# One copy of the 7x7 filter band from HBM per channel group instead of two, and the second half of the partitions filled by VectorE

## The chip, the cores and the metric

The kernel runs on one NeuronCore of one Trainium2 chip. The metric is device time in microseconds of the whole program, from its first to its last instruction. Three runs of the kernel before took 5907.85, 5908.91 and 5926.22 us; the median is 5908.91 us. The profiled execution, from which all lines below come, spans 5915.1 us at a mean granted TensorE clock of 0.979 of full speed.

## The reference

Two convolution blocks in float32 on x of shape 8 x 96 x 96 x 192 (batch, height, width, channels), each with a group norm in front and a residual around it. The change touches the depthwise 7x7 convolution of the second block only.

```
# layer 0
x = x + _L0_conv_ref(_gn(x), ...)   # 192->384 projection, 3x3 depthwise, 4 scans, layer norm, 384->192
# layer 1
x = x + _L1_conv_ref(_gn(x), ...)

def _L1_conv_ref(x, dw_kernel, dw_bias, ...):
    y = conv(x, dw_kernel, SAME, feature_group_count=192) + dw_bias   # 7x7, one filter per channel
    y = (y - mean(y)) * rsqrt(var(y) + 1e-6) * ln_gamma + ln_beta     # over channels
    y = gelu(y @ w0 + b0) @ w1 + b1
    return y * gamma
def _gn(v):   # 32 groups of 6 channels, mean and variance over height, width, group
```

## The kernel before

The program runs as five stages, each with pools of its own, which hand their results on through HBM: A (group norm and projection), B (3x3 convolution and scans), C (layer norm, output projection, residual, statistics of the second group norm), D (the 7x7 convolution), E (layer norm, two-layer perceptron, residual). Only stage D is changed. It lasts from about 2938 us, where its first loads are issued, to about 3459 us, where stage E reads its result.

Stage D computes the convolution as matmuls against a banded matrix. A row of the image tensor X1_d in HBM is a pair of image row and width phase (width modulo PH = 3). A window of HB = 21 image rows times 3 phases gives KB = 63 partitions to contract over. Six such windows (NB) overlap so that each yields 15 image rows, 45 partitions of output. They sit in two halves of the 128 partitions: windows with g = 0 in partitions 0 to 63, those with g = 1 in 64 to 127, three of each (NT). The filter of each channel is laid out beforehand, in HBM tensor Z2_d, as a band of 64 rows and ZW = 208 columns; three 64-column slices of it (d = 0, 1, 2) are the stationary matrices. **The same band serves both halves[...], so the band has to lie in both halves.**

The 192 channels are 32 groups m of HC = 6 channels. `load_d(m)` issues the loads of one group: six DMAs of 384 KB for `xin` (line 753), of which the three with g = 0 go to SyncE's queue and those with g = 1 to GpSimd's, and two DMAs of 312 KB for `band` (line 758), one on each queue, which read the same bytes of Z2_d. `scale_d(m)` applies the second group norm to `xin` in place with eight VectorE instructions (line 1015). `conv_d` takes a pair of groups, m = 2i and 2i + 1 (k = 0 and 1 in the code), and runs channel by channel: 36 matmuls (3 windows t, 3 slices d, 2 groups k, 2 halves g), each of which the profile records as two, and then four ScalarE instructions that move the sums from PSUM to `yo` with the bias added (line 1041). `store_d` writes a finished pair to Y_d (line 1067): the half of group k = 0 by SyncE's queue, that of k = 1 by GpSimd's.

The order is written by hand (`tc.manual_schedule()`). For pair i it is: stores of pair i - 1 for k = 0; loads of groups 2i + 3 and 2i + 4; stores of pair i - 1 for k = 1; scaling of groups 2i + 2 and 2i + 3; the matmuls of pair i. There are five buffers each for `xin` and `band` (ND = 5), so group 2i + 3 takes the buffers of group 2i - 2 and can be read only when pair i - 1 is computed. There are two buffers `yo`, so the sums of pair i can be moved only when the stores of pair i - 2 have landed. Group 0 is read while stage C still ends, groups 1 and 2 at the start of stage D.

Of the kernel before, what the change touches and what calls it, by code (L numbers as in the profile page):

```python
# [84 lines left out]
def conv_blocks_kernel(  # L85
# [31 lines left out]
    nc = tc.nc  # L117
# [26 lines left out]
    HC = GS  # L144
# [19 lines left out]
    Z2_d = dram.tile([64, D, ZW], F32, name="Z2_d")  # L164
# [58 lines left out]
    with ExitStack() as ph:  # L223
# [247 lines left out]
        with tc.manual_schedule():  # L471
# [13 lines left out]
            for b in range(B):  # L485
                more = b + 1 < B
                for t in range(n_t):
# [28 lines left out]
                    k, j = divmod(t, NJ)  # L516
# [27 lines left out]
    with ExitStack() as ph:  # L544
# [13 lines left out]
        def load_b(k):  # L558
            c = slice(k * CC, (k + 1) * CC)
            band = bp_.tile([128, CC, 3, RB], F32, tag="band", name=f"band0_{k}")  # L560
            pin = bp_.tile([128, CC, GB, NJ, S], F32, tag="pin", name=f"pin_{k}")
            for g in range(NG):
                p = g * 64
                nc.sync.dma_start(
                    band[p : p + RB + 4].rearrange("p c t o -> p (c t o)"),
                    ZB_d[:, c].rearrange("r c t o -> r (c t o)"),
                )
                for lo, hi in ((0, RB), (RB, RB + 1), (RB + 1, RB + 2)):
                    nc.sync.dma_start(
                        pin[p + lo : p + hi].rearrange("p c b j h -> p c (b j h)"),  # L570
                        P_d[g, c, lo:hi].rearrange("c r b j h -> r c (b j h)"),
                    )
            return band, pin
# [71 lines left out]
        with tc.manual_schedule():  # L645
            loads = [load_b(k) for k in range(3)]
# [8 lines left out]
            for n in range(NI * (n_k + 1)):  # L655
                k, i = divmod(n, NI)
                z = None
                if k < n_k:
                    if i == 0:
                        band, pin = loads.pop(0)  # L660
# [79 lines left out]
    def load_d(m):  # L740
        c = m * HC
        row = D * WV * B
        pool = d_pools[m % ND > 0]
        xin = pool.tile([128, NT, BP, HC, 2 * WV], F32, tag="xin", name="xin")

        for t in range(NT):
            for g, eng in enumerate((nc.sync, nc.gpsimd)):
                src = bass.AP(
                    tensor=X1_d.tensor,
                    offset=X1_d.offset + (2 * t + g) * HG * PH * row + c * WV * B,  # L750
                    ap=[[row, 64], [1, HC * WV * B]],
                )
                eng.dma_start(
                    xin[g * 64 : (g + 1) * 64, t].rearrange("q a c n -> q (a c n)"), src
                )
        band = pool.tile([128, HC, ZW], F32, tag="band", name="band1")
        for g, eng in enumerate((nc.sync, nc.gpsimd)):
            eng.dma_start(
                band[g * 64 : (g + 1) * 64].rearrange("q c l -> q (c l)"),
                Z2_d[:, c : c + HC].rearrange("r c l -> r (c l)"),  # L760
            )
        return band, xin

    s1 = s1_pool.enter_context(tc.tile_pool(name="s1", bufs=1)).tile(
# [2 lines left out]
    with ExitStack() as ph:  # L767
# [179 lines left out]
        with tc.manual_schedule():  # L947
            load_weights()
            for u in range(n_u + 1):
# [22 lines left out]
                if held is not None:  # L972
                    k, t = divmod(u - 1, n_c)
# [8 lines left out]

            stores.pop(0)()
            first_d = load_d(0)
            for store in stores:
                store()
# [10 lines left out]
    with ExitStack() as ph:  # L997
        cp = ph.enter_context(tc.tile_pool(name="d_const", bufs=1))
        d_pools[1] = ph.enter_context(tc.tile_pool(name="d_in", bufs=ND - 1))
        op = ph.enter_context(tc.tile_pool(name="d_out", bufs=2))  # L1000
        ps_y = ph.enter_context(tc.tile_pool(name="d_ps", bufs=4, space=PSUM))

        dwb = cp.tile([128, D // CD, HC], F32, name="dwb")
        for k in range(2):
            nc.scalar.dma_start(
                dwb[k * 64 : (k + 1) * 64],
                dw_bias.rearrange("(i k c) -> k i c", k=2, c=HC)[k].partition_broadcast(64),
            )

        def scale_d(m, xin):  # L1010
            xv = xin.rearrange("q t a c (v b) -> q t a c v b", b=2)
            for b in range(B):
                sc, sh = (s1[:, a, b % 2, b // 2, m : m + 1] for a in range(2))
                xw = xv[:, :, b // 2, :, :, b % 2]
                nc.vector.tensor_scalar(xw, xw, sc, sh, ALU.mult, ALU.add)  # L1015

        def conv_d(pair, c, yo, i):

            pys = [
                [ps_y.tile([128, 2, BP, 2 * WV], F32, tag=f"py{a}", name=f"py{a}")  # L1020
                 for _ in range(2)]
                for a in range(2)
            ]
            for t in range(NT):
                for n, d in enumerate((1, 0, 2)):
                    lo, hi = 2 * max(0, 1 - d), 2 * (WV - max(0, d - 1))
                    for k in range(2):
                        for g in range(2):
                            rows = slice(g * 64, g * 64 + KB)
                            nc.tensor.matmul(  # L1030
                                pys[t // 2][g][k * 64 : (k + 1) * 64, t % 2, :, lo:hi],
                                pair[k][0][rows, c, d * ZS : d * ZS + 64],
                                pair[k][1][rows, t, :, c, lo + 2 * (d - 1) : hi + 2 * (d - 1)],
                                start=(n == 0),
                                stop=(n == 2),
                            )
                if t == 0:
                    continue
                for g in range(2):
                    bl = slice(g, 4 + g, 2) if t == 1 else slice(4 + g, 5 + g)  # L1040
                    nc.scalar.activation(
                        yo[:, bl, :, c],
                        pys[t // 2][g][:, : 2 - t // 2].rearrange("q t b (a v) -> q t (b a) v", a=NV),
                        AF.Identity,
                        bias=dwb[:, i, c : c + 1],
                        scale=1.0,
                    )

        def store_d(yo, i, k):

            eng = (nc.sync, nc.gpsimd)[k]

            w = BP * NV * HC * 2 * WQ
            n = NV * HC * 2 * WQ if i == D // CD - 1 else w
            for at in range(0, w, n):
                for bl in range(NB):

                    pieces = [(3, HB - 3)]
                    if bl == 0:
                        pieces.append((HB - 3, HB))  # L1060
                    if bl == NB - 1:
                        pieces.append((0, 3))
                    for lo, hi in pieces:
                        r = (S - HB - bl * HG) * PH
                        src = yo[k * 64 + lo * PH : k * 64 + hi * PH, bl]
                        dst = Y_d[r + lo * PH : r + hi * PH, 2 * i + k]
                        eng.dma_start(  # L1067
                            dst.rearrange("r b a c n -> r (b a c n)")[:, at : at + n],
                            src.rearrange("r a c n -> r (a c n)")[:, at : at + n],
                        )  # L1070

        n_i = D // CD
        with tc.manual_schedule():
            loads = [first_d] + [load_d(m) for m in range(1, 3)]
            make_weights(ps_y.tile([128, 512], F32, tag="py1", name="ps_b0"))
            for m in range(2):
                scale_d(m, loads[m][1])
            done = None
            for i in range(n_i):
                pair, loads = loads[:2], loads[2:]  # L1080

                if done is not None:
                    store_d(done, i - 1, 0)
                for m in (2 * i + 3, 2 * i + 4):
                    if m < 2 * n_i:
                        loads.append(load_d(m))
                if done is not None:
                    store_d(done, i - 1, 1)
                if i + 1 < n_i:
                    for k in range(2):  # L1090
                        scale_d(2 * i + 2 + k, loads[k][1])
                done = op.tile([128, NB, BP * NV, HC, 2 * WQ], F32, tag="yo", name=f"yo_{i}")
                for c in range(HC):
                    conv_d(pair, c, done, i)
            for k in range(2):
                store_d(done, n_i - 1, k)
# [246 lines left out]
```

## Time and profile before

| Stage | us | PE busy | VectorE busy | GpSimd busy | mean DMA share | GB/s |
|---|---|---|---|---|---|---|
| A, 0 to 780 | 780 | 712.77 | 412.96 | 111.33 | 0.85 | 245 |
| B, 780 to 1835 | 1055 | 1027.33 | 988.04 | 826.14 | 0.91 | 237 |
| C, 1835 to 2938 | 1103 | 1075.60 | 762.03 | 723.69 | 0.87 | 256 |
| D, 2938 to 3459 | 521 | 417.81 | 166.28 | 149.23 | 0.95 | 303 |
| E, 3459 to 5915 | 2456 | 2417.89 | 1125.46 | 751.17 | 0.27 | 70 |

The numbers are the busy time of each engine in a stretch of the span, in us. The DMA share is the mean busy share of the core's 16 DMA engines and the last column what they moved. In four of the five stages TensorE is busy for more than nine tenths of the time. In stage D it is busy for 418 of 521 us, and the DMA engines are the busiest resource. Stage D is 8.8% of the span, and a hundredth of the whole time is 59 us, so what can be won or lost there is small against the whole.

### The profile page before, as it was taken

What the parts mean: (1) busy time and instruction counts of PE and PEld (TensorE: products, weight loads), DVE (VectorE), ACT (ScalarE), POOL (GpSimd) and SP (SyncE); (2) the same over time, 40 slices, a digit from 0 to 9 for tenths busy, and PEclk for the clock granted to TensorE, in tenths of its full rate; (3) what the DMA queues carried; (4) which work ended last, traced back from release to release, by engine and by line L of the source; (5) the groups of instructions that cost most, each with busy time, mean ns of one, the idle gap of its engine ahead of it and who ended that gap; (6) DMA issues with size and microseconds to landing.
All of it is one profiled execution on the core that took longest, in us unless ns stands there. A gap on an engine that the chain in (4) does not pass through costs nothing.

```text
span 5915.1 us, 122868 instructions
## 1 busy us (share of the span) xinstructions
PE 5651.4 (96%) x48550; PEld 3971.6 (67%) x48550; DVE 3454.8 (58%) x8023; ACT 2429.1 (41%) x6146; POOL 2561.6 (43%) x2731
## 2 busy tenths in 40 slices
PE   6999989999998999999878869999999999999999
PEld 3655533333335989898767757777777777777777
DVE  5555459999996667777733334444444444444443
ACT  2444447777775555555434322222222222222221
POOL 1111138888886666666522223323333333333332
PEclk9999989999999999999989989999999999999999
DMA  7999779999997889888899952232323232323221
GB/s 205 279 284 262 217 211 244 244 245 244 243 243 201 256 262 267 262 266 262 240 317 332 316 130 74 63 77 64 80 65 81 64 80 65 80 60 81 63 65 39
DMA packets 634283, 1054.49 MB, mean 178 GB/s; under 512 B 108683, under 2 KB 509284, under 8 KB 633708
## 3 DMA queue, kind: packets, MB, share of 16 engines
q1 hardware_dynamic: 516924, 620.81, 40.3%
q0 software_dynamic: 110656, 423.20, 22.0%
q8 instruction: 384, 6.29, 0.5%
q10 hardware_dynamic: 6128, 2.61, 0.2%
q14 instruction: 191, 1.56, 0.1%
HBM read 585.19 MB, written 476.72 MB: 180 GB/s over the span
## 4 chain that ended last, share of the span: by engine, by line
PE 78%; DMA 5%; issue 1%; DVE 1%; POOL 1%; SPq 0%; ACT 0%; ACTq 0%; POOLq 0%; DVEq 0%
PE po L1232 19%; PE po L835 14%; PE hp L1202 12%; PE pl L582 10%; PE hp L1212 7%; PE pa L603 5%; PE pt L833 4%; PE py L1030 3%; DMA xin<-X_d 3%; PE pa L606 2%; PE pt L1185 2%; DMA Y_d<-yo 2%; DMA X_d<-x1c 0%; DMA P_d<-po 0%; SPq L1067 0%
## 5 line engine op out<-in xcount | busy, mean ns | idle before, releaser
L1221 ACT ACTIVATE g<-hp,b0g 128x384 f32<-128x384 f32 x1152 | 564.4, 589 | 1830.5 <-PE hp L1212 1830.5
L1232 PE MATMUL po<-w1g,g 128*128 128x192 f32 x6912 | 1160.0, 327 | 0.0
L1232 PEld LDWEIGHTS po<-w1g,g 128*128 128x128 f32 x6912 | 1118.8, 190 | 1.1 <-issue 1.1
L835 PE MATMUL po<-wc,mt 128*96 128x193 f32 x4608 | 912.8, 333 | 0.0
L1189 DVE COPY yT<-pt 128x384 f32<-128x384 f32 x288 | 251.0, 871 | 1043.3 <-PE pt L1185 1043.1
L1202 PE MATMUL hp<-yT,w0w 128*128 128x384 f32 x2304 | 781.4, 489 | 0.4 <-DVE yT L1189 0.4
L835 PEld LDWEIGHTS po<-wc,mt 128*96 128x96 f32 x4608 | 701.8, 163 | 68.2 <-ACT mean L839 64.8
L1250 POOL DMA_DIRECT2D out_dram<-xo x576 | 342.9, 597 | 875.4 <-DVE xo L1239 860.6
L582 PE MATMUL pl<-pin,band 34*32 34x380 f32 (+1 forms) x13824 | 629.7, 489 | 18.5 <-DMA pin<-P_d 18.5
L1202 PEld LDWEIGHTS hp<-yT,w0w 128*128 128x128 f32 x2304 | 429.5, 191 | 257.2 <-issue 3.2
L612 DVE TENSOR_TENSOR_SCAN z<-decay,loc 128x768 f32<-128x768 f32 x288 | 505.9, 1757 | 60.1 <-ACT loc L591 30.7
L652 POOL TENSOR_TENSOR mo<-mo,z 128x768 f32<-128x768 f32 x288 | 530.1, 1841 | 3.4 <-ACT mo L607 0.4
L29 POOL TENSOR_TENSOR rs<-rs_ve,neg_half 96x8 f32<-96x8 f32 x96 | 159.2, 1659 | 824.1 <-DVE rs_ve L28 804.0
L582 PEld LDWEIGHTS pl<-pin,band 34*32 34x32 f32 x13824 | 232.7, 107 | 397.5 <-issue 396.2
L621 DVE TENSOR_TENSOR_SCAN z<-decay,z 128x768 f32<-128x768 f32 x288 | 498.3, 1730 | 0.0
L1030 PE MATMUL py<-xin,band 63*64 63x248 f32 (+1 forms) x6912 | 409.5, 392 | 74.7 <-DVE xin L1015 46.3
L842 ACT ACTIVATE sq<-pt,mean 96x384 f32<-96x384 f32 x768 | 443.5, 578 | 25.7 <-ACT mean L839 0.8
L1030 PEld LDWEIGHTS py<-xin,band 63*64 63x64 f32 x6912 | 354.4, 141 | 129.5 <-DVE xin L1015 36.5
L603 PE MATMUL pa<-loc,mix 128*32 128x384 f32 x3456 | 431.9, 493 | 0.0
L606 PE MATMUL pa<-last,down 96*32 96x384 f32 x1152 | 426.8, 493 | 1.0 <-ACT mo L607 1.0
L1212 PE MATMUL hp<-yT,w0w 64*128 64x384 f32 x2304 | 423.5, 500 | 0.0
L365 PE MATMUL pm<-xT,win 128*128 128x384 f32 x1152 | 395.8, 494 | 5.2 <-DVE po L389 5.2
(116 smaller groups left out, 7621.5 us busy)
## 6 DMA issues: line engine op xcount, KB each, us to landing
P_d<-po POOLq DMA_DIRECT2D x96, 1152.0 KB, 9.6
pin<-P_d SPq DMA_DIRECT2D x192, 576.0 KB
mt<-M_d SPq DMA_DIRECT2D x576, 192.0 KB
xq<-in_x_dram SPq DMA_DIRECT2D x96, 576.0 KB
xr<-in_x_dram SPq DMA_DIRECT2D x384, 144.0 KB
X_d<-x1u POOLq DMA_DIRECT2D x192, 288.0 KB, 4.2
X_d<-x1c SPq DMA_DIRECT2D x192, 288.0 KB
y<-Y_d SPq DMA_DIRECT2D x24, 2304.0 KB
```

The lines of the kernel that those rows point to most:

```text
L582: nc.tensor.matmul(pls[g][at * RB : (at + 1) * RB, :, lo:hi], band[rows, c, kh, :], pin[rows, c, :, NJ - 1 - j, lo + kh - 1 : hi + kh - 1] ...
L603: nc.tensor.matmul(pa[at], mix[:, i, at], loc[:, q], start=True, stop=True)
L606: nc.tensor.matmul(pa[at], down[:, to], last[:, q], start=True, stop=True)
L612: nc.vector.tensor_tensor_scan(zf, decay_f, loc.rearrange("p q n -> p (q n)"), 0.0, ALU.mult, ALU.add)
L621: nc.vector.tensor_tensor_scan(zr, decay_f, zr, 0.0, ALU.mult, ALU.add)
L652: nc.gpsimd.tensor_tensor(m, m, z, ALU.add)
L835: nc.tensor.matmul(po[:S, b], lhs[m], wc[:, m], start=(m == 0), stop=(m == NC - 1))
L1030: nc.tensor.matmul(pys[t // 2][g][k * 64 : (k + 1) * 64, t % 2, :, lo:hi], pair[k][0][rows, c, d * ZS : d * ZS + 64], pair[k][1][rows, t, ...
L1202: nc.tensor.matmul(hps[m, q], w0w[:, 2 * q, m * 128 : (m + 1) * 128], yT[:, 2 * q], start=True, stop=False,)
L1212: nc.tensor.matmul(hps[m, q], w0w[p, 1, m * 128 : (m + 1) * 128], yT[p, 1], start=False, stop=True,)
L1221: nc.scalar.activation(g[:, m, q], hps[m, q], AF.Gelu, bias=b0g[:, m : m + 1], scale=1.0)
L1232: nc.tensor.matmul(po[:, q], g[:, m, q, k * 128 : (k + 1) * 128], w1g[:, m], start=(m == 0), stop=(m == NE - 1),)
```

## The change

Of the two DMAs for a group's band, one is left: group m reads it into the half g = m % 2, on that half's queue, so that even groups use SyncE's queue and odd groups GpSimd's and each queue carries one band per pair. The other half is filled by one VectorE copy of 64 partitions by 1248 elements, ahead of the scaling of that group. The purpose is to read each band from HBM once and to load both queues alike.

```diff
         band = pool.tile([128, HC, ZW], F32, tag="band", name="band1")
-        for g, eng in enumerate((nc.sync, nc.gpsimd)):
-            eng.dma_start(
-                band[g * 64 : (g + 1) * 64].rearrange("q c l -> q (c l)"),
-                Z2_d[:, c : c + HC].rearrange("r c l -> r (c l)"),
-            )
+
+        g = m % 2
+        (nc.sync, nc.gpsimd)[g].dma_start(
+            band[g * 64 : (g + 1) * 64].rearrange("q c l -> q (c l)"),
+            Z2_d[:, c : c + HC].rearrange("r c l -> r (c l)"),
+        )
         return band, xin
...
-        def scale_d(m, xin):
+        def scale_d(m, band, xin):
+            g = m % 2
+            nc.vector.tensor_copy(
+                band[(1 - g) * 64 : (2 - g) * 64], band[g * 64 : (g + 1) * 64]
+            )
             xv = xin.rearrange("q t a c (v b) -> q t a c v b", b=2)
...
-                scale_d(m, loads[m][1])
+                scale_d(m, *loads[m])
...
-                        scale_d(2 * i + 2 + k, loads[k][1])
+                        scale_d(2 * i + 2 + k, *loads[k])
```

## The prediction

> **What bounds the kernel now.** I first split the span into stretches, to find what limits the 7x7 stage, which alone is changed. The columns are length, busy time of each engine (with instruction counts), granted clock, DMA share, GB/s.
>
> ```profile
> 3050.00:3100.00 50.00, 44.22 (x761) 40.22 (x757) 18.41 (x31) 21.47 (x42) 14.39 (x28) 0.93 1.00 339
> 3100.00:3150.00 50.00, 45.67 (x800) 38.39 (x796) 15.21 (x26) 23.82 (x47) 14.61 (x27) 0.93 1.00 336
> 3300.00:3350.00 50.00, 42.91 (x694) 35.27 (x690) 13.22 (x23) 20.62 (x41) 14.06 (x26) 0.90 1.01 312
> 3400.00:3450.00 50.00, 41.41 (x714) 39.67 (x706) 4.74 (x8) 22.53 (x44) 12.47 (x25) 0.91 0.56 165
> ```
>
> The DMA engines are busy without a break (share 1.00) until the loads run out near 3400; PE, at 43 to 46 of 50 us, is next. VectorE has over 30 us free in each 50. So bytes set the pace, and PE is close behind. The second view is TensorE in order of time: start, length, records, and in brackets the idle time before.
>
> ```profile
> 2965.72 1.19 PE L1030 MATMUL py<-xin,band 63*64 63x256 f32 x4 [6.49 <-DVE xin L1015]
> 2981.80 49.24 PE L1030 MATMUL py<-xin,band 63*64 63x256 f32 x864 [14.89 <-DVE xin L1015]
> 3036.36 25.63 PE L1030 MATMUL py<-xin,band 63*64 63x256 f32 x432 [5.33 <-DVE xin L1015]
> 3064.12 25.44 PE L1030 MATMUL py<-xin,band 63*64 63x256 f32 x432 [2.13 <-DVE xin L1015]
> 3093.21 24.52 PE L1030 MATMUL py<-xin,band 63*64 63x256 f32 x432 [3.65 <-DVE xin L1015]
> ...
> 3368.38 25.41 PE L1030 MATMUL py<-xin,band 63*64 63x256 f32 x432 [5.54 <-ACT yo L1041]
> 3398.36 32.96 PE L1030 MATMUL py<-xin,band 63*64 63x256 f32 x567 [4.57 <-ACT yo L1041]
> ```
>
> One pair of groups is 6912/16 = 432 records. Pairs 0 and 1 run as one block (49.24 us, 24.6 each), since their data is there. From pair 2 on PE stops in every pair, first for scaled inputs, from pair 9 on mostly for ScalarE. The idle times of this view from 2981.8 on add up to 53.4 us: all that a faster supply could win. The period of a pair is that from pair 2 at 3036.36 to pair 15 at about 3415.6 (3398.36 plus the 292 records left of pair 14 at some 59 ns): 379.2/13 = 29.17 us. Third, who waits for whom (total us, times, longest):
>
> ```profile
> DVE xin L1015 <- DMA Y_d<-yo: 174.8, 11, 19.6
> DVE xin L1015 <- DMA xin<-X_d: 89.2, 16, 16.6
> ACT yo L1041 <- DMA xin<-X_d: 78.1, 8, 11.9
> PE py L1030 <- DVE xin L1015: 46.3, 13, 14.9
> PE py L1030 <- ACT yo L1041: 23.7, 6, 5.5
> ```
>
> PE waits for VectorE, VectorE for DMAs. ScalarE neither reads xin nor writes it; I read its wait for a DMA as one for the store of pair i - 2 out of its buffer yo, put down to whatever landed last. Both are waits for one DMA pool.
>
> **What the Trainium skill says.** "VectorE: DVE Perf Modes", section "The perf-mode tier table": an fp32 copy from SBUF to SBUF runs at two elements a cycle, 1227 ns for 2048. That is 1067 ns of streaming and 160 fixed. The trace of before has no contiguous copy of this kind; the nearest, the weight scaling of 128x768, three of which take 1.67 us or 557 ns from start to start, agrees (768/1.92 + 160 = 560 ns). "SBUF — State Buffer", section "Who interferes with whom": such a copy shuts GpSimd out of a shared port, also while it writes DMA descriptors. No line of before shows it; a GpSimd DMA issue takes about 510 ns here. "DMA: Bandwidth & Descriptors", section "Rules for kernel authors": transfers to two halves of the partitions share the same 16 DMA engines. The trace agrees: two queues are open and the share stands at 1.00. So dropping one half's band saves its bytes in full, on whichever queue it was.
>
> **The change part by part.** *Removed:* 32 of these 64 DMAs.
>
> ```profile
> xin<-X_d POOLq DMA_DIRECT2D x94, 384.0 KB, 14.0
> Y_d<-yo POOLq DMA_DIRECT2D x90, 270.0 KB, 13.6
> band<-Z_d SPq DMA_DIRECT2D x32, 312.0 KB
> band<-Z_d POOLq DMA_DIRECT2D x32, 312.0 KB, 16.9
> ```
>
> A group reads 6 x 384 + 2 x 312 = 2928 KB and writes 6 x 270 + 2 x 54 = 1728 KB (the 54 KB pieces are the image's edge rows), so a pair moves 9312 KB. At 29.17 us that is 327 GB/s, within the 312 to 339 of the stretches. Now it moves 8688 KB, 0.933 of it. If the DMA engines stay the limit at the same rate, the period becomes 27.22 us, still above PE's 24.6 to 25.6; the saving is 1.95 us in each of 13 periods, **25.4 us**. After pair 15 nothing is read, so the tail only moves earlier. The 32 issues (about 0.5 us each) go too, beside a full DMA queue: nothing.
>
> *Added:* 32 copies of 64x1248. By the page 1248/1.92 + 160 = 810 ns; at one element a cycle (the scaling here, 576 strided elements in 666 ns) it would be about 1360 ns. I take 0.81: 26 us in all, 43 at the other end, in a stage where VectorE is idle for some 350 us. On its own path it is one link: loads land, copy, scaling (4.75 us for eight), PE. While DMA is the limit a link of 0.8 us costs nothing, because the queued stores and loads of another group keep the DMA engines busy meanwhile.
>
> *The new wait:* the copy stands ahead of the scaling and waits for the band, which is issued after its group's xin. Behind it on VectorE queue the eight scalings, and for those PE. For odd groups in the steady state the band is on GpSimd's queue, whose loads come before its stores, while half of xin on SyncE's queue comes after 1728 KB of stores, so xin is last: nothing. For even groups the band closes SyncE's loads, some 2 us later than xin; they are scaled a whole pair ahead (3039.39 for pair 3, which starts at 3064.12): nothing. Only the start has no slack. Group 1's xin had landed at 2976.8 and scaling began at 2976.95. Its band, 312 KB on one queue at half of some 320 GB/s, comes about 2.0 us later; with the copy, PE starts pair 0 some **2.8 us later**. Against that, groups 1 to 5, which pair 2 waits for, bring 5 x 312 KB less, 4.9 us at 327 GB/s; but pair 0's end, which lets group 5 be read, comes later by the 2.8, and the DMA engines run dry in between. For pair 2 I count a net loss of 1.4 us, the middle between nothing and the 2.8.
>
> *GpSimd locked out:* at most 0.8 us per copy for an issue that has a full queue behind it: nothing.
>
> **Sum:** -25.4 + 1.4 = -24.0; 5908.9 - 24.0 = **5885 us**.
>
> **The rivals.** (1) *Supply still limits, but less well overlapped.* When PE and DMA are nearly level, a wait for a buffer idles both: PE must finish a pair before the next loads start, and yo is freed only by stores queued behind loads. For it: from pair 9 on PE waits for ScalarE at rates of 312 to 318 GB/s, so order already costs something. If PE keeps about 2.6 us of idle time per pair on 25.5, the period is 28.1 us and the gain 13 x 1.07 - 1.4 = 12.5: **5896 us**. Against it: the share of 1.00, a full queue, even then. (2) *The late waits vanish.* With fewer bytes before them the stores land in time and the later pairs run at the 336 GB/s of the stretches around 3100: 8688 KB in 26.5 us, a gain of 13 x 2.67 = 34.7, less 1.4: **5876 us**. For it: pairs 2 to 8 did so. Against it: nothing shows what set off the change at pair 9. (3) *The copy takes the place of the read.* If the pace is set by the chain of load, copy, scaling and PE, and fewer bytes bring no group earlier, then one copy per pair (0.81 to 1.36) lies on it: 15 x 1.1 + 2.8 = 19 us more, **5928 us**. For it: PE's commonest wait is for the scaling. Against it: that scaling itself waits 12 to 20 us for DMAs.
>
> **How the numbers follow.** Forecast 0.57, rival 1 0.20, rival 2 0.17, rival 3 0.06. The bound of 0.3% is 17.7 us. Faster: nearly all of the forecast (0.53), rival 2 (0.17) and a little of rival 1 (0.03), 0.73. Within: most of rival 1 and the rest, 0.22. Slower: 0.05. The range, 5870 to 5900, takes in the forecast, rival 2 and the better half of rival 1, and the two ends of the copy's price (at 1.36 us only the start moves, by 0.5 us); it leaves out rival 3 and the far ends of 1 and 2.
>
> **What would show it.** Right: stage D shorter by some 24 us and no other stage changed; DMA share near 1.00 to the end of the loads; a period near 27.2 us; PE's idle time down to some 30 us; the copy near 0.8 us; first long block of PE at about 2984.6. Rival 1 shows in a DMA share below 0.97 in mid-stage, rival 2 in the loss of waits for ScalarE, rival 3 in VectorE waiting for band rather than xin. I am wrong if the rate in GB/s falls with the bytes: then requests, not bytes, were the limit.

## The result and the profile after

The changed kernel takes 5881.5 us (median of 4 runs, 5878.4 to 5886.1) against 5912.6 us before (4 runs, 5907.9 to 5926.2) in the same comparison. The ratio is 0.9944, with a 95% interval of 0.9925 to 0.9963: some 31 us less. The profiled execution spans 5881.8 us, 33.3 us less than the one of before. All but about 1 us of that lies in the 7x7 stage: stages A, B and C together end 1.3 us earlier, and stage E takes as long as before.

The same four stretches as in the prediction, in the columns length, busy times, granted clock, DMA share, GB/s:

```profile
3050.00:3100.00 50.00, 45.28 (x796) 41.12 (x792) 21.56 (x35) 23.13 (x44) 15.77 (x28) 0.93 0.98 336
3100.00:3150.00 50.00, 45.00 (x824) 38.36 (x820) 22.19 (x36) 23.01 (x44) 16.15 (x28) 0.97 0.98 332
...
3300.00:3350.00 50.00, 46.54 (x812) 38.02 (x812) 20.10 (x33) 22.80 (x44) 15.21 (x28) 0.97 0.99 326
...
3400.00:3450.00 50.00, 11.12 (x205) 7.66 (x197) 5.62 (x20) 6.52 (x13) 17.84 (x33) 0.65 0.75 174
```

In the first three stretches the DMA engines are still busy nearly all the time, at 326 to 336 GB/s, where before the rate fell to 312 late in the stage. The last stretch is already past the end of the convolution. TensorE in order of time, with the idle time before each block in brackets:

```profile
2981.96 43.71 PE L1035 MATMUL py<-xin,band 63*64 63x256 f32 x789 [15.47 <-issue]
3026.27 4.45 PE L1035 MATMUL py<-xin,band 63*64 63x256 f32 x75 [0.60 <-issue]
3035.14 25.23 PE L1035 MATMUL py<-xin,band 63*64 63x256 f32 x432 [4.42 <-DVE xin L1020]
...
3248.99 48.69 PE L1035 MATMUL py<-xin,band 63*64 63x256 f32 x864 [3.95 <-DVE xin L1020]
...
3356.83 24.81 PE L1035 MATMUL py<-xin,band 63*64 63x256 f32 x432 [3.64 <-DVE xin L1020]
3383.08 8.33 PE L1035 MATMUL py<-xin,band 63*64 63x256 f32 x148 [1.44 <-DVE xin L1020]
3394.02 16.70 PE L1035 MATMUL py<-xin,band 63*64 63x248 f32 x280 [2.61 <-issue]
```

Pair 2 starts at 3035.14 and pair 15 at 3383.08, so the period is 347.94/13 = 26.76 us, 2.41 us less than the 29.17 of before; 13 of them are 31.3 us. The block of 864 records shows two pairs that ran on without a stop. The idle times from the first block on add up to 38.7 us, against 53.4. Who waits for whom:

```profile
DVE band L1013 <- DMA band<-Z_d: 127.5, 29, 11.8
DVE xin L1020 <- DMA Y_d<-yo: 106.9, 13, 10.2
...
PE py L1035 <- DVE xin L1020: 32.8, 11, 7.5
...
PE py L1035 <- ACT yo L1046: 0.2, 1, 0.2
```

VectorE's long wait is now split: first for the band, then, once it has copied, for the rest of xin (the line names a store, but what the scaling needs is xin). TensorE's wait for ScalarE, 23.7 us before, is gone. The copy itself, with the shortest, median and longest duration in ns:

```profile
L1013 DVE COPY band<-band x32: 802/805/879, 2959.7 to 3371.8; 64x1248 f32<-64x1248 f32 x32
```

### The profile page after: what moved, and what is told of

It reads as the page before. It is cut to its first block, busy times and chain, and to the rows that moved or that the text cites. A ratio compares the mean times of both kernels' runs of the same rounds, so it can differ in the third digit from the quotient of the medians.

```text
span 5881.8 us, 122840 instructions
## 1 busy us (share of the span) xinstructions
PE 5632.6 (96%) x48550; PEld 3954.1 (67%) x48550; DVE 3480.6 (59%) x8055; ACT 2431.2 (41%) x6146; POOL 2556.9 (43%) x2715
## 4 chain that ended last, share of the span: by engine, by line
PE 77%; DMA 6%; issue 1%; DVE 1%; POOL 1%; ACT 0%; SPq 0%; POOLq 0%; ACTq 0%; DVEq 0%
PE po L1237 19%; PE po L836 14%; PE hp L1207 12%; PE pl L582 10%; PE hp L1217 7%; PE pa L603 5%; PE pt L834 4%; DMA Y_d<-yo 3%; PE pa L606 2%; PE pt L1190 2%; DMA xin<-X_d 2%; PE py L1035 2%; DVE xin L1020 0%; DMA band<-Z_d 0%; DMA X_d<-x1c 0%
## 5 line engine op out<-in xcount | busy, mean ns | idle before, releaser
L1035 PE MATMUL py<-xin,band 63*64 63x248 f32 (+1 forms) x6912 | 391.2, 382 | 61.6 <-DVE xin L1020 32.8
L1035 PEld LDWEIGHTS py<-xin,band 63*64 63x64 f32 x6912 | 337.1, 137 | 115.4 <-DVE xin L1020 43.1
```

The costliest lines, as they stand in the source:

```text
L1035: nc.tensor.matmul(pys[t // 2][g][k * 64 : (k + 1) * 64, t % 2, :, lo:hi], pair[k][0][rows, c, d * ZS : d * ZS + 64], pair[k][1][rows, t, ...
```

## The experiments

The questions were whether the copy is really hidden, whether the bytes alone explain the gain, and what the even sharing of the queues is worth. Medians are given with the ratio to the kernel before and its 95% interval; the kernel before had a median of 5913.7 to 5919.9 us in these comparisons.

**e1, the copy alone.**

```diff
-        (nc.sync, nc.gpsimd)[g].dma_start(band half g)
+        for g, eng in enumerate((nc.sync, nc.gpsimd)):
+            eng.dma_start(band half g)        # both halves, as before; copy kept
```

> The copy alone: both halves of the band are still read from HBM, and the VectorE copy is done as well (it writes the same bytes again). The bytes theory (the gain is the 312 KB per group no longer read; the copy is hidden): as before within 3 us, pair period 29 to 30 us, waits of ScalarE for late stores in the later pairs as before. The chain theory (the copy lies on the path of load, scaling, matmul): 15 copies of 0.81 us, 12 us slower than before. If the gain came from the order that the copy brings in rather than from the bytes: as fast as the changed kernel, some 31 us below before.

5913.7 us, ratio 1.0002 (0.9994 to 1.0010). The copy and its wait cost nothing at these bytes, and bring nothing. Its period, from pair 2 at 3038.14 to pair 15 at 3414.07, is 28.92 us; the late waits for ScalarE that I had expected again are not in this profile, so the same bytes can be moved without them, and without being faster.

**e2, two DMAs of half the size.**

```diff
-        (nc.sync, nc.gpsimd)[g].dma_start(band[half g], Z2_d[:, c : c + HC])
+        for j, eng in enumerate((nc.sync, nc.gpsimd)):
+            eng.dma_start(band[half g, j * h : (j + 1) * h], Z2_d[:, c + j * h : c + (j + 1) * h])   # h = HC // 2
```

> As the changed kernel, but the one band DMA of 312 KB is issued as two of 156 KB, three channels each, one on each queue: bytes as after, number of DMAs as before. Bytes theory: as the changed kernel, 31 us below before, within 4 us. Rival, that the number of DMAs in flight or to be issued sets the pace: as before, ratio 1.000. The queues are level here within each group too.

5903.7 us, ratio 0.9982 (0.9975 to 0.9990): a third of the gain. Neither expectation holds. The bytes are those of the changed kernel, and two thirds of what they should have brought is missing.

**e3, all bands on SyncE's queue.**

```diff
-        (nc.sync, nc.gpsimd)[g].dma_start(
+        nc.sync.dma_start(
```

> As the changed kernel, but all bands are read on SyncE's queue (into the half g of the group, as before), so that per pair SyncE's queue carries 4656 KB and GpSimd's 4032. Bytes theory with one shared set of DMA engines: 24 to 31 us below before, the queues' sharing matters little. Rival, that each queue has half of the rate and the fuller one sets the pace: 4656 KB at 167 GB/s is 28.5 us per pair against 26.8, 22 us of the gain gone, some 8 us below before.

5904.0 us, ratio 0.9980 (0.9972 to 0.9989). Nearer to the rival. Here is its steady part as one stretch, in the columns as above:

```profile
3050.00:3340.00 290.00, 257.17 (x4564) 235.24 (x4556) 114.88 (x185) 134.24 (x256) 81.84 (x147) 0.96 0.98 323
```

and that of the changed kernel:

```profile
3050.00:3340.00 290.00, 264.00 (x4710) 229.18 (x4706) 122.47 (x197) 135.99 (x260) 91.61 (x161) 0.96 0.99 332
```

The DMA share hardly tells them apart (0.98 and 0.99), the rate does: 323 against 332 GB/s. I counted the trace's DMA packets in steps of 0.25 us over 290 us of the steady part and took a queue as working when more than three of its packets were in flight. In the changed kernel both queues work for 97% of the time, at 333 GB/s. In e3 they do for 89%, at 335 GB/s; for 9% SyncE's works alone, at 206 GB/s, and for 2% GpSimd's alone, at 204. So e3's mean is about 0.89 x 335 + 0.11 x 206 = 321.

Is it the queue that is slow alone, or the half? In this stage every DMA reaches at most 64 partitions, all in one half. Stage A of the changed kernel tells the two apart: there GpSimd's queue stores tiles of all 128 partitions, at times with no other queue at work. From 450.75 to 461.00 us (q0 is GpSimd's queue; packets, MB, share of the 16 engines):

```profile
DMA packets 811, 3.53 MB, mean 345 GB/s; under 512 B 44, under 2 KB 44, under 8 KB 811
q0 software_dynamic: 811, 3.53, 99.3%
```

So a single queue can move 345 GB/s. The 204 to 206 belong to a queue that works alone on the 64 partitions of one half.

**e4, the copy twice.**

```diff
+            for _ in range(2):
                 nc.vector.tensor_copy(band[other half], band[half g])
```

> As the changed kernel, but each copy is done twice: 32 more VectorE copies of 0.81 us. If the copy is hidden behind the DMA traffic: as the changed kernel within 3 us. If one copy per pair lies on the path of load, copy, scaling, matmul: 14 x 0.81 = 11 us slower than the changed kernel, and the single copy of the change costs as much. A part of it would mean that PE and DMA take turns as the limit.

5881.7 us, ratio 0.9942 (0.9930 to 0.9955), the same as the changed kernel. The copy is off the path. Its odd bands come early on GpSimd's queue and are copied while VectorE waits for xin.

**e5, all bands on SyncE's queue, copy after the scaling.**

```diff
-        (nc.sync, nc.gpsimd)[g].dma_start(
+        nc.sync.dma_start(
...
-            nc.vector.tensor_copy(...)        # ahead of the eight scalings
+            nc.vector.tensor_copy(...)        # behind them
```

> As the kernel with all bands on SyncE's queue (5904 us), but the copy is done after the eight scalings of its group, not ahead of them. Theory of place (what cost that kernel 22 us is that an odd group's band lands behind pair i - 1's stores and behind xin, and that copy and scaling begin only then): now only the copy of 0.8 us follows the band, which lands some 2 us after xin while the scaling takes 4.75 us, so the loss goes: 5882 to 5886, as the changed kernel. Rival, that SyncE's queue is fuller (4656 against 4032 KB per pair): stays at 5904.

5894.4 us, ratio 0.9957 (0.9944 to 0.9971): about 10 us better than e3, about 13 short of the changed kernel by the medians. The place of the wait and the fuller queue both count. SyncE's queue is still alone for about 10% of the time.

**e6, the halves swapped.**

```diff
-        g = m % 2
+        g = 1 - m % 2          # in load_d and scale_d
```

> As the changed kernel, but with the turns swapped: even groups read the band on GpSimd's queue into partitions 64 to 127, odd groups on SyncE's into 0 to 63. Bytes, number of DMAs and share of each queue per pair are those of the changed kernel. Theory of place: the odd group is the one that the next pair waits for, and its band is again behind the stores, so 15 to 22 us slower than the changed kernel, about 5900. Theory of level queues: as the changed kernel, 5882.

5894.6 us, ratio 0.9962 (0.9949 to 0.9974). Same bytes, same number, same share of each queue, 13 us slower by the medians (the intervals of the ratios just overlap with that of e4, which equals the changed kernel). What is left to differ is that the odd group, which the next pair waits for, gets its band behind the stores. Both queues work together for only some 93% of the time, probably since TensorE frees buffers later.

**e7, all bands on GpSimd's queue.**

```diff
-        (nc.sync, nc.gpsimd)[g].dma_start(
+        nc.gpsimd.dma_start(
```

> As the changed kernel, but all bands are read on GpSimd's queue, whose loads come ahead of its stores: queues as uneven as with all on SyncE's (GpSimd's 4656 KB, SyncE's 4032). Theory of place: the odd group's band comes early and SyncE's queue has less ahead of its half of xin, so as the changed kernel or up to 5 us faster, 5877 to 5884. Theory of level queues: as with all on SyncE's queue, 5904.

5920.6 us, ratio 1.0009 (1.0001 to 1.0017): the whole gain is lost, and neither theory had that. Its steady part:

```profile
3050.00:3340.00 290.00, 246.66 (x4160) 200.50 (x4156) 109.61 (x177) 118.43 (x231) 85.59 (x153) 0.92 0.98 296
```

The share is 0.98 again, the rate 296 GB/s. GpSimd's queue is alone for only some 5% of the time; with both at work the rate is no more than 298. Something other than a dry queue slows them here. The trace shows a part of it. The packets of a band are told by their size (4992 bytes against 6144), so those that GpSimd's queue writes into partitions 0 to 63 can be counted: they are in flight for 15% of the time, nearly always while SyncE's queue loads xin into the same 64 partitions, and then both queues together move 242 GB/s, against 306 for the rest. As an estimate from these figures, at 306 the same bytes would have taken some 9 us less of these 290. e3 crosses halves as well, but there the crossing band mostly runs while GpSimd's queue stores, and 383 GB/s are moved.

**e8, the odd group's loads ahead of the stores.**

```diff
-                if done is not None:
-                    store_d(done, i - 1, 0)
                 for m in (2 * i + 3, 2 * i + 4):
                     if m < 2 * n_i:
                         loads.append(load_d(m))
-                if done is not None:
-                    store_d(done, i - 1, 1)
+                    if m == 2 * i + 3 and done is not None:
+                        store_d(done, i - 1, 0)
+                        store_d(done, i - 1, 1)
```

> As the changed kernel, but the loads of the odd group 2i + 3 are issued ahead of the stores of pair i - 1 on SyncE's queue too, and both halves of the stores ahead of group 2i + 4. Asks what is left as the limit. If the chain of stores, loads, scaling still holds the next pair up, 1728 KB leave it (some 10 us) and the period falls from 26.8 toward what TensorE takes, 25 us: up to 20 us faster than the changed kernel, 5862 to 5875. If bytes are the limit: the same as the changed kernel within 4 us. If the stores are then late for ScalarE: slower.

5897.9 us, ratio 0.9965 (0.9953 to 0.9978), 16 us slower than the changed kernel by the medians. The shorter chain does not pay. The steady part runs at 314 GB/s with a DMA share of 1.00. The order in which each queue was given its DMAs tells its load packets from its store packets. Here both queues load at once for about 55% of the time, at 282 GB/s, and both store for 26%, at 374. In the changed kernel they do so for only 16%, at 300, and for 72% one loads while the other stores, at some 346. The kernel before shows the same two levels, 28% of the time at 291 and 56% at 338. Two stretches of the changed kernel, the first with loads on both queues, the second with loads on SyncE's and stores on GpSimd's, in the columns as above:

```profile
3152.35:3157.95 5.60, 5.60 (x115) 4.86 (x108) 0.81 (x1) 2.21 (x5) 1.88 (x3) 1.00 1.03 307
3104.35:3114.25 9.90, 9.90 (x192) 8.58 (x188) 4.87 (x8) 5.50 (x11) 1.17 (x3) 1.00 0.93 340
```

One of e8 with loads on both:

```profile
3143.85:3161.55 17.70, 17.29 (x283) 14.99 (x279) 1.05 (x2) 6.92 (x14) 5.09 (x9) 0.90 1.02 262
```

So loads beside loads are slower than loads beside stores, and e8's order brings more of the slow kind. Why they are slower is not shown.

**e9 and e10, all bands on one queue, but into that queue's own half.**

```diff
-        g = m % 2
+        g = 1                  # e9: GpSimd's queue, partitions 64 to 127
+        g = 0                  # e10: SyncE's queue, partitions 0 to 63
```

> As the kernel with all bands on GpSimd's queue (5920.6 us, where the even bands go into partitions 0 to 63, the half that SyncE's loads fill), but every band is read into partitions 64 to 127, the half of GpSimd's own loads. If that kernel lost because two queues wrote one half at once: 10 to 30 us faster than it, 5890 to 5910. If it lost because GpSimd's queue carries 4656 KB per pair and SyncE's 4032, which then runs dry or frees yo late: the same, 5920 within 5 us.

> As the kernel with all bands on SyncE's queue (5904 us, where the odd bands go into partitions 64 to 127), but every band is read into partitions 0 to 63, the half of SyncE's own loads. Crossing theory: faster, 5885 to 5895. Theory of level queues (GpSimd's queue runs dry for a tenth of the time, and SyncE's alone moves only some 205 GB/s): the same as that kernel, 5904 within 5 us.

e9 takes 5899.1 us, ratio 0.9973 (0.9962 to 0.9984), 21 us faster than e7. e10 takes 5902.9 us, ratio 0.9981 (0.9973 to 0.9989), the same as e3. So with all bands on one queue the kernel lands near 5900 whichever queue it is, unless GpSimd's queue writes into the half that SyncE's fills. In both a queue is alone on its half for about 9% of the time (e9: GpSimd's, at 225 GB/s; e10: SyncE's, at 207).

**e11, the stores of k = 0 on ScalarE's queue.**

```diff
-            eng = (nc.sync, nc.gpsimd)[k]
+            eng = (nc.scalar, nc.gpsimd)[k]
```

> As the changed kernel, but the stores of group k = 0 go out on ScalarE's queue, which holds nothing else, so that SyncE's queue holds loads alone and three queues share the DMA engines. If the number of queues with work limits the rate (one alone some 205 GB/s, two 335): period from 26.8 toward TensorE's 25, up to 20 us faster than the changed kernel, 5862 to 5875. If the engines are full with two queues: as the changed kernel within 4 us. If ScalarE is held up by issuing, or loads in step on two queues slow each other: up to 15 us slower.

6005.4 us, ratio 1.0148 (1.0134 to 1.0162), far slower than any expectation. ScalarE has to issue the stores itself and is held while it does so; behind that wait the moves of the next sums out of PSUM, and TensorE behind those. A part of its order of time:

```profile
3116.73 16.32 ACTq L1072 DMA_DIRECT2D Y_d<-yo  x7
3133.53 3.88 ACT L1046 ACTIVATE yo<-py,dwb 128x512 f32<-128x512 f32 x8 [16.44 <-DMA xin<-X_d]
```

Seven issues take 16.3 us. Whether a third queue would raise the rate can't be read from this time.

**e12, half of the band.** Three of six channels use another channel's filter here.

```diff
-            band[g * 64 : (g + 1) * 64], Z2_d[:, c : c + HC]
+            band[g * 64 : (g + 1) * 64, :h], Z2_d[:, c : c + h]      # h = HC // 2
...
+            nc.vector.tensor_copy(band[half g, h:], band[half g, :h])
             nc.vector.tensor_copy(band[other half], band[half g])
```

> As the changed kernel, but only the bands of the first three channels of a group are read (156 KB instead of 312) and VectorE copies them to the place of the other three, so half of the channels are computed with another channel's filter. Queues stay level and the odd band stays on GpSimd's queue; a pair moves 8376 KB instead of 8688. If bytes are what is left as the limit at this order: period 26.76 x 0.964 = 25.8 us, 13 us faster than the changed kernel, about 5869. If TensorE is the floor by now: 5872 to 5880. If bytes no longer count and the chain of load, copy, scaling does: the same, 5882, or a few us slower for the third copy.

5871.4 us, ratio 0.9927 (0.9914 to 0.9941), 10 us below the changed kernel by the medians where bytes alone would give 13. With queues level and the odd band in its place, fewer bytes still make the stage shorter. TensorE comes close behind (5871.4 lies just below the 5872 to 5880 expected for TensorE as the floor): five of its blocks are double pairs, such as

```profile
3187.86 48.77 PE L1040 MATMUL py<-xin,band 63*64 63x256 f32 x864 [2.70 <-DVE xin L1025]
3240.95 48.01 PE L1040 MATMUL py<-xin,band 63*64 63x256 f32 x864 [4.32 <-DVE xin L1025]
3293.60 48.81 PE L1040 MATMUL py<-xin,band 63*64 63x256 f32 x864 [4.63 <-DVE xin L1025]
```

## Why the prediction held, and where its reasons did not

*The limit.* The stage was bound by its transfers with TensorE next. e1 and e12 fit that: the copy without the saved bytes brings nothing, and another 312 KB less per pair brings about 10 us more.

*The copy.* Forecast 0.81 us, measured 0.805 (median), and hidden: e1's interval leaves room for a cost of 6 us at most, and the runs of e4, with every copy done twice (5877.4 to 5885.5 us), lie where those of the changed kernel lie. The price from the page "VectorE: DVE Perf Modes" of the Trainium skill, which no row of before could confirm for a copy, fits within 1%. The row that I set beside it was misread: the three weight scalings took 612 ns each and started 530 ns apart; 557 is only a third of their total.

*The sign of rival 3.* VectorE's longest wait is now the one for the band (127.5 us), which I had named as the sign that the copy lies on the path. The sign was badly chosen. For odd groups a wait for the rest of xin follows the copy and hides it:

```profile
3074.25 0.81 DVE L1013 COPY band<-band 64x1248 f32<-64x1248 f32 x1 [5.61 <-DMA band<-Z_d]
3083.53 4.75 DVE L1020 TENSOR_SCALAR xin<-xin,s 128x576 f32<-128x576 f32 x8 [8.47 <-DMA Y_d<-yo]
```

For even groups the band does come last, by 2 to 3 us, but they are scaled a pair ahead; e4 finds no cost.

*GpSimd locked out.* No cost shows: its band issues take 517 ns at the median, as before (519).

*The saving in the steady state.* Forecast 25.4 us in 13 periods, measured 31.3. The term that was too small is the period: the bytes went down by the forecast 6.7%, but the rate did not stay at 327 GB/s, it rose to 332 (8688 KB in 26.76 us). Pairs 2 to 8 fell from 28.3 to 26.6 us, which is about the ratio of the bytes; pairs 9 to 14, which before stopped for ScalarE too, fell from about 30.1 to 27.0. That second part is rival 2, which I had given 0.17. The late stops are not a fixed cost of the kernel before, though: e1, with the same bytes, shows none, moves 330 GB/s (9312 KB in 28.92 us) and is no faster. What set them off stays open.

*The start.* Forecast a net loss of 1.4 us for pair 2; it starts 1.2 us earlier, about as much as stage C happens to end earlier in this execution (its last matmul group of that stage starts at 2924.8 instead of 2926.0), so the loss is about zero. The step that failed is the band of group 1: I had it land 2.0 us after xin, at 2978.8, and the copy began at 2976.28, with xin. The first long block starts at 2981.96, not at 2984.6.

*The wait behind the copy.* I had called it free in the steady state because the odd group's band comes first on GpSimd's queue and even groups have a pair's time in hand. e6 fits that: with the odd band behind the stores some 13 us go.

*The step that was wrong.* "Dropping one half's band saves its bytes in full, on whichever queue it was." I took this from the page "DMA: Bandwidth & Descriptors", section "Rules for kernel authors", by which transfers to two halves share the same engines and several queues bring no bandwidth, and from a DMA share of 1.00. Five kernels with the saved bytes but other queues (e2, e3, e7, e9, e10) brought between none and half of the gain. The measurement decides: one queue by itself moved 204 to 225 GB/s in these traces (e3, e9, e10), two together 326 to 335. It was alone on one half of the partitions then; in stage A one queue alone on all 128 moved 345, so what the page says of queues is not refuted, but two transfers to different halves did not stand in each other's way here. When one queue carries 624 KB per pair more than the other, that much is moved with the other queue dry: 3.1 us at 206 GB/s instead of 1.9 at 335, a loss of 1.2 us per pair or, as an estimate, some 16 us in 13, of the size that e3, e9 and e10 lost (18 to 22 us). My forecast came out right because the change keeps the queues level and puts the odd band on the right one. The first of these was a purpose of the change, but the prediction gave it no worth, and in that it was lucky.

*What was forecast as a sign.* Share near 1.00: 0.98 to 1.00. Period 27.2: 26.76. TensorE's idle time some 30 us: 38.7. The prediction let only the stops shrink. They shrank by 14.7 us between the two profiles, and TensorE's busy time, which it took as fixed, by 18.3 (409.5 to 391.2). That the sum was near the forecast is luck in this respect. The shorter busy time does not make the gain by itself, for e3, some 22 us slower than the changed kernel, has 392.6 us of it and 53.4 us of stops; why it fell is open.

*What stays open.* Why loads on both queues at once move less than loads beside stores (282 to 300 against some 346 GB/s). In e7 the loads of both queues into one half explain, by the estimate above, about half of the 21 us that e9 wins back; the rest is not accounted for. e2, which crosses halves on both queues, shows both cases (237 to 274 GB/s where GpSimd's queue crosses while SyncE's loads, 369 where SyncE's crosses while GpSimd's stores), but its loss was not taken apart further. No version here is faster than the changed kernel and computes the whole result.

## What to carry to other kernels

A DMA share of 1.00 says that something is always in flight, not that the engines move what they can; compare GB/s, count how long each queue is alone on its half of the partitions, and look at what runs beside what, loads beside loads or loads beside stores. When bytes were taken away from this transfer-bound loop, it paid in full only where both queues lost alike and where the band that the next step waits for stood early in its queue; of the 31 us gained here, other placements of the same bytes kept between nothing and some 20. A copy on an idle engine was free where it started on data that arrive before the last piece, or had a pair's time in hand.

## What the runs showed of the hardware that I had not expected

One DMA queue alone on 64 partitions moved 204 to 225 GB/s (SyncE's and GpSimd's alike, short stretches between others), two queues on the two halves up to 337 together. The queue itself is not the bound: on 128 partitions GpSimd's alone moved 345.

With both queues at work, loads on both moved 282 to 300 GB/s (the changed kernel, before, e8), and loads on one beside stores on the other some 338 to 346 (the changed kernel and before).

TensorE's busy time for the same 6912 matmul records (their ends are modelled) lay between 387.5 us (e12) and 411.0 us (e11), with 409.5 before and 391.2 in the changed kernel. The granted clock was 0.93 before and 0.97 in the changed kernel in the stretch from 3100 to 3150. The shape and number of the matmuls are the same; no run tells why it differs.
